# Two fused attention layers on one core: weight products, an early query and loads at two handovers put in another order

## The chip, the cores and the metric

The kernel runs on one core of a Trainium2 chip. A core has four compute engines that matter here: TensorE (PE) for matmuls, VectorE (DVE) and ScalarE (ACT) for elementwise work, GpSimd (POOL) for some elementwise work beside them; SyncE (SP) issues the transfers, which sixteen DMA engines carry out. Each engine works through its own queue of instructions in order, and semaphores make it wait for others. On-chip memory is SBUF, matmuls write to PSUM, and inputs, outputs and what is kept between stages lie in HBM.

The metric is the device time of one execution in microseconds (us), as the median of the runs. Lower is better.

## The reference, cut to what matters

The input x is 8 images of 256 channels with 64 by 64 pixels, all in float32. Two layers follow each other.

```
# layer 0
xr   = conv(x, w_sr, stride 4, 4x4 kernel)            # 256 channels, 16x16
xr   = (xr - mean_c) / sqrt(var_c + eps) * g + b      # over channels
q    = w_q x ; k, v = split(w_kv xr)                  # 8 heads of 32
x    = x + gamma * w_out softmax(q k^T / sqrt(32)) v  # 4096 queries, 256 keys

# layer 1
qkv  = w_qkv x                                        # 768 channels
agg  = grouped_1x1(depthwise_5x5(qkv))                # 96 groups of 8 channels
ms   = concat(qkv, agg)                               # heads of 3 x 8 channels
q, k = relu(ms.q), relu(ms.k) ; v = [ms.v, 1]
att  = q (k^T v) ; att = att[:-1] / (att[-1] + eps)   # linear attention, per head
x    = x + batchnorm(w_proj att)
```

## The kernel before, in words

The work is written for a tile framework: the program asks for tiles out of pools (a tag and a number of buffers say when a tile's memory is reused), and the framework's scheduler sets the order of the instructions on each engine and the semaphores between them. So the order in the source is a wish, and the built order can differ: independent work is pulled ahead. Where the memory of an earlier pass is taken again by a later one, the first use of it waits for the last use before it, transfers included. All transfers of the kernel are issued on SP's one queue; a transfer waits, besides for its data and its place, for the landing of the transfer eight places before it.

There are three passes, which hand their results on through HBM.

**The first pass** (`first_pass`) does layer 0 and the qkv product of layer 1. Its loop runs over steps n, 32 for each image: a strip of 512 pixels (`NG` = 8 for each image), a half of the channels, a half of the keys. A step computes scores on PE (L784) and their exponentials on ACT (L790), the values (`valued`, L808), the sum of the two key halves on POOL (`joined`, L819), the denominators (`counted`, L824), and `normed` on DVE: a transpose `rden` (L836), a reciprocal, a transpose `rall` (L839) and the product `att` (L841). `added` multiplies by the output weights (PE, L856), adds x (DVE, L857) and stores x. Every second strip `differences` and seven `qkv` products (PE, L900) follow, whose results are taken out of PSUM by DVE (`part`, `whole`, `stage`) and stored as k, v and `planes`. `keys_values` (L694 to L760) is a generator: it does the strided convolution with weights `wsr`, the normalisation (mean, var, rs) and keys and values; for the first image it runs before the loop, for the others in pieces within the image before. `queries` (L769, L777) makes q for a strip and a half: two matmuls and a copy by ACT.

`conv_weights` is another generator. It makes the weights of the second pass: for each of four groups it loads `wd` (L668), adds (L670), and makes eight products `wb` (L674, DVE, 128 x 1536) with one buffer, each of which is stored to HBM (`wt`). Each call of `next(weights, None)` makes one product, 32 in all. `border(b)` stores zeros to the rims of v in HBM, four transfers for each image.

**The second pass** (`second_pass`) does the depthwise and pointwise part as matmuls, and the sums k^T v. It runs over 64 units (t, k, b). A unit loads weights `w` (`load_weights`, L1130), pixels `d` (`load_cells`, L1136), and tokens `kq` and `vq` (`load_tokens`, L1143 and L1153). `paired` makes differences `c` of d (two on DVE, L1163 and L1164, and a copy on POOL, L1167). `convolve(u, 1, i)` is L1227 with d's of k and v, `convolve(u, 0, i)` is L1231 for q; ACT copies one of three banks to `both` (L1234), DVE adds it to the others (`s`, L1243), ACT makes `r` (L1244). `positive` is the relu of kq (L1210), `summed_raw` (L1253) and `summed` (L1270) are the sums, `ended` and `spread` (L1313 to L1330) turn them into the block matrix `bd`, `applied` (L1344 to L1356) makes the attention of agg, `stored` (L1364) stores it. `taps` are the weights with which `summed` is multiplied; taps_0 is for units of t = 0 (the first 32), taps_1 for t = 1.

**The third pass** (`third_pass`) makes the attention of qkv and the projection, in 64 steps. `loads(n)` loads raw pixels (L1473), x (L1482) and at some steps sums and agg (L1450, L1493); `vec` (L1515) and `wproj` (L1517) are loaded once. `flat` is a relu by ACT (L1506), `applied` is n (PE, L1541), den and tok (DVE, L1546), `turned` is a transpose on PE (L1559) with a copy by ACT (L1560), `proj` is p (PE, L1577), z (ACT, L1586) and y (DVE, L1595).

A check of the softmax's sums at the first pass's end decides whether a slower, general program has to run behind the third pass; it doesn't for these inputs.

The functions that the diff touches, and what calls them:

## Time and profile before

| | us |
|---|---|
| runs of the kernel | 3958.32, 3962.27, 3964.38 (median 3962.27) |
| the profiled execution | 3960.62 |
| its span | 3958.8 |
| PE busy | 3876.3 |
| VectorE busy | 2271.4 |
| ScalarE busy | 1517.6 |
| GpSimd busy | 1296.6 |
| first pass, roughly | 0 to 2076 |
| second pass, roughly | 2035 to 3303 |
| third pass, roughly | 3289 to the end |

The passes overlap by some work. The profile is that of one execution; a busy share is an average over all three passes, so what one edit is worth is read from the waits and windows around its own place. The profile's windows give, for a stretch of time, the busy time of each engine, the clock granted to PE as a share of the full one, and how busy the DMA engines were.

### The profile page before, as it was taken

Reading aid. Unit: us, or ns where it says so; the run is one execution under the profiler, and the core shown is the slowest. Engines: PE = TensorE matmul, PEld = TensorE weight load, DVE = VectorE, ACT = ScalarE, POOL = GpSimd, SP = SyncE. Lnnn points to the kernel's source line nnn. Section 1 sums busy time; section 2 is a strip of 40 time slices with the busy share of each in tenths; the row PEclk is TensorE's granted clock in tenths of the full one; section 3 lists DMA queues with packets and bytes.
Section 4 is the critical chain, followed back from the end, with each engine's and each line's share of the span. In section 5 each row is a group of like instructions: output and inputs, shape, how many; then the busy total and the mean of one; then the engine's idle time right before and its main releaser. Section 6 shows DMA issues by size and latency. Waiting matters only on the chain. (4 is left out here: it accounts for less than half of the span.)

```text
span 3958.8 us, 70047 instructions
## 1 busy us (share of the span) xinstructions
PE 3876.3 (98%) x27074; PEld 2277.0 (58%) x27074; DVE 2271.4 (57%) x3752; ACT 1517.6 (38%) x3473; POOL 1296.6 (33%) x1394
## 2 busy tenths in 40 slices
PE   8999999999999999999998999999999998999998
PEld 4443534434344343443346888888888885555555
DVE  3667465564655646556674666666666664444443
ACT  2344344443444434444432222222222223544444
POOL 2334343343433424334433444444444440000000
PEclk9999999999999999999998999999999999999999
DMA  7656354353443534444549887878778747777774
GB/s 246 188 176 201 101 140 129 96 154 99 136 132 98 149 104 129 136 115 116 135 117 265 247 225 221 231 221 229 230 214 230 206 144 198 225 210 222 209 223 141
DMA packets 570039, 691.35 MB, mean 175 GB/s; under 512 B 60128, under 2 KB 429280, under 8 KB 565600
## 3 DMA queue, kind: packets, MB, share of 16 engines
q1 hardware_dynamic: 569696, 686.78, 60.8%
q8 instruction: 215, 3.52, 0.4%
q14 instruction: 128, 1.05, 0.1%
HBM read 412.54 MB, written 274.10 MB: 173 GB/s over the span
## 5 line engine op out<-in xcount | busy, mean ns | idle before, releaser
L819 POOL TENSOR_TENSOR e<-e,e 128x512 f32<-128x512 f32 x512 | 682.1, 1364 | 931.5 <-PE av L808 864.1
L790 ACT ACTIVATE e<-sc 128x512 f32<-128x512 f32 x1024 | 531.0, 602 | 799.1 <-PE sc L784 794.4
L1227 PE MATMUL cv<-w,c 128*128 128x128 f32 x3072 | 386.9, 280 | 10.9 <-POOL c L1167 10.5
L1227 PEld LDWEIGHTS cv<-w,c 128*128 128x128 f32 x3072 | 361.2, 193 | 41.4 <-issue 29.3
L1595 DVE TENSOR_TENSOR y<-z,xs 128x256 f32<-128x256 f32 x256 | 142.7, 644 | 323.7 <-ACT z L1586 303.7
L784 PE MATMUL sc<-q,kk 32*128 32x512 f32 x2048 | 318.5, 640 | 1.5 <-DVE part L969 1.0
L1270 PE MATMUL sums<-vq,r 128*32 128x288 f32 x4096 | 307.3, 411 | 0.1
L900 PE MATMUL qkv<-differences,combined 128*128 128x512 f32 x576 | 304.8, 620 | 0.9 <-ACT e L790 0.7
L916 DVE TENSOR_TENSOR whole<-part,qkv 128x512 f32<-128x512 f32 x256 | 175.3, 687 | 189.3 <-PE qkv L900 179.0
L1244 ACT ACTIVATE r<-s 128x512 f32<-128x512 f32 x256 | 160.9, 628 | 306.8 <-DVE s L1243 300.0
L808 PE MATMUL av<-e,vv 128*32 128x512 f32 x2048 | 272.7, 604 | 1.9 <-ACT att L828 1.9
L1577 PE MATMUL p<-att,wproj 128*128 128x512 f32 x512 | 249.7, 610 | 9.6 <-DMA wproj<-in_w_proj_dram 5.6
L1586 ACT ACTIVATE z<-p,bn 128x256 f32<-128x256 f32 x256 | 133.8, 578 | 314.4 <-PE p L1577 240.7
L1231 PE MATMUL cv<-c,w 128*128 128x128 f32 x2048 | 253.1, 277 | 1.0 <-DVE s L1243 1.0
L856 PE MATMUL o<-att,wout 128*128 128x512 f32 x512 | 234.9, 600 | 10.8 <-DVE att L841 10.8
L769 PE MATMUL q<-x,wq 128*128 128x512 f32 x512 | 244.3, 599 | 0.0
L697 PE MATMUL sr<-x,wsr 128*128 128x256 f32 x1024 | 234.7, 384 | 8.4 <-DMA wsr<-in_w_sr_dram 8.4
L1577 PE MATMUL p<-agg,wproj 128*128 128x512 f32 x512 | 242.3, 595 | 0.0
L1231 PEld LDWEIGHTS cv<-c,w 128*128 128x128 f32 x2048 | 239.5, 192 | 1.2 <-DVE s L1243 1.2
L697 PEld LDWEIGHTS sr<-x,wsr 128*128 128x128 f32 x1024 | 196.5, 192 | 61.6 <-issue 33.8
L1234 ACT COPY both<-cv 128x512 f32<-128x512 f32 x128 | 75.0, 586 | 409.0 <-PE cv L1227 355.5
L1243 DVE TENSOR_TENSOR s<-cv,both 128x512 f32<-128x512 f32 x256 | 172.1, 672 | 86.4 <-PE cv L1231 43.3
(143 smaller groups left out, 6031.6 us busy)
## 6 DMA issues: line engine op xcount, KB each, us to landing
vq<-v SPq DMA_DIRECT2D x256, 384.0 KB
planes<-stage SPq DMA_DIRECT2D x128, 578.0 KB
d<-planes SPq DMA_DIRECT2D x128, 578.0 KB
raw<-planes SPq DMA_DIRECT2D x128, 272.0 KB
x<-in_xp_dram SPq DMA_DIRECT2D x64, 512.0 KB
wsr<-in_w_sr_dram SPq DMA_DIRECT2D x128, 256.0 KB
x<-x SPq DMA_DIRECT2D x128, 256.0 KB
k<-turned SPq DMA_DIRECT2D x256, 128.0 KB
```

The costliest lines, as they stand in the source:

```text
L697: nc.tensor.matmul(ps[:, oc], w[:, ci, oc * P : (oc + 1) * P], strips(b, f // 2)[:, ci, f % 2 * NK : (f % 2 + 1) * NK], start=(f == ci == ...
L769: nc.tensor.matmul(ps, consts["wq"][:, ci, c * P : (c + 1) * P], strips(b, s)[:, ci], start=(ci == 0), stop=(ci == 1),)
L784: nc.tensor.matmul(scs[h], kks[b][rows, c, kc * P : (kc + 1) * P], qs[rows], start=True, stop=True)
L790: nc.scalar.activation(e, scs[h], AF.Exp, scale=D0**-0.5)
L808: nc.tensor.matmul(sums["av"][cols], vvs[b][:, kc, c * P + h * D0 : c * P + (h + 1) * D0], es[h], start=(kc == 0), stop=(kc == 1),)
L819: nc.gpsimd.tensor_tensor(es1[h], es0[h], es1[h], ALU.add)
L856: nc.tensor.matmul(ps, consts["wout"][:, c, oc * P : (oc + 1) * P], att[c], start=(c == 0), stop=(c == 1))
L900: nc.tensor.matmul(ps, w, x, start=True, stop=True)
L1227: nc.tensor.matmul(out, x, m, start=(da == 0), stop=(da == 1))
L1231: nc.tensor.matmul(out, m, x, start=(da == 0), stop=(da == 1))
L1270: nc.tensor.matmul(ps[h * D0 : (h + 1) * D0, : 36 * D1].rearrange("p (r n e) -> p r n e", r=3, e=D1), kt[:, par, h, 2 * r + c], vq[:, r : ...
L1577: nc.tensor.matmul(ps.rearrange("p (f q n) -> p f q n", f=4, q=4), wproj[:, j, oc * P : (oc + 1) * P], src, start=(j == 0), stop=(j == 3),)
```

## The change

Four places are changed.

- In the first pass the queries of strip 0's second half are made within the chain of the first keys, between two pieces of `keys_values`, and no longer in the loop's step 0.
- `next(weights)` is called in steps above 32 where n % 8 is 3 or 6, and no longer in each of steps 0 to 31. The zeros of image 0 are asked for at step 20 instead of 2.
- At the second pass's start the loads of w0 (four), of taps_1 and of unit 2's tokens move from ahead of the loop, and the loop's first lines, to unit 0 behind `load_cells(2, 1)`.
- In the third pass the pools for data and flattened tiles are asked for ahead of the pool of constants, so each gets another place in memory.

In the order as built, 24 of the 32 weight products stand in the steps of image 0 and eight in those of image 1, where before all 32 stood in image 0. On SP the second pass begins d0_0, d1_2, kq_2, vq_2 (four), w0 (four), taps_1; before, it began taps_1, w0 (four), d0_0, d1_2, a w1, kq_2, vq_2 (four). On DVE the `c` of unit 6 stands behind two `s` of unit 2 that it stood ahead of. vec and wproj are issued between the last two loads of d while the second pass still runs, and no longer between its last two stores of attention; on PE the first two matmuls of n for step 1 stand ahead of the first p.

```diff
-    first = queries(0, 0, 0)
+    q = {0: queries(0, 0, 0)}
+    next(ahead)
+    q[1] = queries(0, 0, 1)
     for _ in ahead:
         pass
...
-    q, es = {0: first}, {}
+    es = {}
...
-        if n < n_all and kc == 0 and n + 2 < n_all:
+        if 0 < n < n_all and kc == 0 and n + 2 < n_all:
             q.pop(n // 2 - 1, None)
             q[n // 2 + 1] = queries(*order[n + 2][:3])
...
-        next(weights, None)
+
+        if n > 32 and n % 8 in (3, 6):
+            next(weights, None)
         if n < n_all:
             b, at = n // 32, n % 32
-            if at == 2:
+            if at == (20 if b == 0 else 2):
                 border(b)
...
     load_tokens(1)
-    for g in range(4):
-        load_weights(0, 0, g)
-
     def load(home, src, name):
...
-    for t in range(2):
+
+    def load_taps(t):
         taps.append((more if t else w_taps).tile([P, 4, 36, D1], F32, tag="taps", name=f"taps_{t}"))
         nc.sync.dma_start(taps[t], a.w_taps[:, 4 * t : 4 * t + 4])
+
+    load_taps(0)
...
-        if 0 < u < n_all - 1:
+        if 1 < u < n_all - 1:
             load_tokens(u + 1)
...
         if u + 2 < n_all:
             load_cells(u + 2, 1)
+        if u == 0:
+            load_tokens(2)
+            for g in range(4):
+                load_weights(0, 0, g)
+            load_taps(1)
...
+    data, flattened = (ctx.enter_context(tc.tile_pool(name=name, bufs=2)) for name in ("data3", "flattened3"))
     const = ctx.enter_context(tc.tile_pool(name="const3", bufs=1))
-    data, flattened, results = (
-        ctx.enter_context(tc.tile_pool(name=name, bufs=2)) for name in ("data3", "flattened3", "results3")
-    )
+    results = ctx.enter_context(tc.tile_pool(name="results3", bufs=2))
```

## The prediction

> **What bounds the kernel now.** I read the page's busy table first, then TensorE's (PE's) waits, then what each engine does around the longest waits, then short windows with clock and DMA share.
>
> ```profile
> span 3958.8 us, 70047 instructions
> PE 3876.3 (98%) x27074; PEld 2277.0 (58%) x27074; DVE 2271.4 (57%) x3752; ACT 1517.6 (38%) x3473; POOL 1296.6 (33%) x1394
> ```
>
> PE is busy 98%. The change takes no matmul away, so all it can win is PE's idle time, 3958.8 − 3876.3 = 82.5 us, and the time that PE works at half clock after a stall. PE's waits:
>
> ```profile
> PE o L856 <- DVE att L841: 10.8, 4, 6.1
> PE cv L1227 <- POOL c L1167: 10.5, 2, 9.5
> PE raw L1253 <- ACT kq L1210: 5.7, 1, 5.7
> PE p L1577 <- DMA wproj<-in_w_proj_dram: 5.6, 1, 5.6
> PE p L1577 <- ACT att L1560: 4.1, 2, 2.9
> PE var L721 <- DVE sq L715: 1.6, 1, 1.6
> ```
>
> The first lies in batch 0 of the first pass; the second and third where the second pass begins; the next two where the third begins; the last in the first keys' chain. In the timeline of VectorE (DVE), which gives start, length, operation and what ended the idle time before it:
>
> ```profile
> 70.74 2.54 DVE L674 TENSOR_TENSOR wb<-wd,wsmall 128x1536 f32<-128x1536 f32 x1 [0.20 <-DMA wt<-wb]
> 79.53 2.27 DVE L674 TENSOR_TENSOR wb<-wd,wsmall 128x1536 f32<-128x1536 f32 x1 [6.25 <-DMA wt<-wb]
> 81.73 0.70 DVE L836 STREAM_TRANSPOSE rden<-den 128x512 f32<-128x512 f32 x1
> 83.57 1.13 DVE L841 TENSOR_TENSOR att<-att,rall 128x512 f32<-128x512 f32 x1
> ...
> 110.28 0.69 DVE L670 TENSOR_TENSOR wd<-wd 128x512 f32<-128x512 f32 x1 [6.87 <-DMA wd<-in_w_big_dram]
> 111.00 1.76 DVE L674 TENSOR_TENSOR wb<-wd,wsmall 128x1536 f32<-128x1536 f32 x1
> 112.68 0.71 DVE L836 STREAM_TRANSPOSE rden<-den 128x512 f32<-128x512 f32 x1
> ```
>
> A weight product `wb` heads DVE's queue, waits there for the store of the one before (one buffer), and holds the softmax's last steps (rden to att) behind it. PE's output matmuls start at 84.75 (3.18 us idle) and 115.27 (6.08 us idle). Windows, whose columns are length, busy time by engine, granted clock, DMA share and GB/s:
>
> ```profile
> 84.70:88.70 4.00, 3.94 (x5) 1.65 (x6) 2.82 (x2) 0.00 (x0) 1.13 (x1) 0.57 0.29 66
> 112.00:120.00 8.00, 4.73 (x6) 1.60 (x6) 5.63 (x8) 2.09 (x7) 0.00 (x0) 0.57 0.48 169
> 2084.00:2100.00 16.00, 6.54 (x62) 6.27 (x63) 3.22 (x4) 1.82 (x3) 4.68 (x6) 0.57 1.02 307
> 3303.00:3315.00 12.00, 6.41 (x17) 3.21 (x18) 1.14 (x5) 2.65 (x6) 0.70 (x1) 0.57 0.65 193
> ```
>
> Each long stall is followed by half clock. At the second pass's start the DMA engines are full (1.02); at the third's they are not (0.65).
>
> **The change, part by part.** The sums are against the profiled execution (3960.62 us); the median of the runs is 3962.27, 1.65 more, and gains carry over.
>
> *First keys' chain.* q[1] is two matmuls (L769, about 0.6 us each) that stood among step 0's scores; they now stand between mean and var, where PE idles 1.65 us. Cover for 1.2 us; ScalarE's (ACT's) copy of q (some 0.6 us) goes ahead of `wide` and may cost 0.2. Gain **1.0** (0 if the copy delays `wide`; 3 if the half clock after this chain, 2.9 us in 44 to 52, goes too).
>
> *Weights and zeros.* The same 4 loads, 4 adds, 32 products (1.76 us alone, up to 2.8 beside POOL) and 32 stores. In the built order 24 products still stand in batch 0 and 8 in batch 1 (before: all 32 in batch 0), so the scheduler still hoists them, but fewer at a time. Between the first two atts the order was two products, now one, so the wait to 79.53 needn't stand before rden: den was ready at 76.73, rden to att takes 3.0, PE would start at about 80–81.6 instead of 84.75. Gain 3.2. The second: the reload of wd no longer stands before the fourth att, but two products do; den was ready at 102.43, two products with a landing between cost 2×1.8 + 4 to 5, so att ends at 111–113 instead of 115.2. Gain 2.3 to 4, I take 3. Against it: products now stand ahead of x and `whole`, which free PSUM banks for qkv; for two of them I charge 1 to 1.5 us each, 2.5 in all. For batch 1, where PE hardly waits today, nothing: DVE is busy 70 of 90 us late in the first pass, the eight products are 14–20 us spread over it; if that cover is missing, each costs its store's landing, up to 4–5 us. The zero stores of batch 0 go on SP ahead of the first wd load, 8 × 0.5 us; wd isn't wanted until the first att at 67: nothing.
>
> Here a rule bears. After the 3.18 us gap, the window 84.70–88.70 was granted 0.57: 43% of 4 us lost, **1.7 us**. The Trainium skill ("TensorE: Matmul & The Clock Gate", Part 1) has the clock halved after at least one idle window of about 3.4 us; by that a gap of 3.18 costs no dip and its end saves 3.2. By the row it saves 3.2 + 1.7 = 4.9. The rule also says that a shorter wait left over elsewhere is free of the dip. I go by the row: sub-3.4 gaps here do dip, so gaps that merely shrink keep theirs. The second gap's dip stays. Batch 0: 4.9 + 3 − 2.5 = **5.5** (0 to 12).
>
> *First to second pass.*
>
> ```profile
> 2081.50 1.07 POOL L1324 TENSOR_TENSOR bd<-rep,pix 128x512 f32<-128x512 f32 x1 [2.80 <-DMA taps<-in_w_taps_dram]
> 2092.52 1.24 POOL L1167 COPY c<-d 128x544 f32<-128x544 f32 x1 [6.54 <-DMA d<-planes]
> 2149.74 0.72 DVE L1163 TENSOR_TENSOR c<-d 128x544 f32<-128x544 f32 x1 [3.28 <-DMA d<-planes]
> ```
>
> taps_1 (0.58 MB) and four w0 loads (1.5 MB) leave their place ahead of d0_0 and d1_2 on SP. The first w0 load waited for all earlier stores to land (issue at 2081.41, 3.7 us after taps_1's) and everything on SP stood behind it; d1_2 went out at 2083.98 and landed at 2092.5. Now d1_2 can go out at about 2076.4: behind stores that land by 2081.4, with d0_0 ahead, 1.16 MB at 0.29 MB/us is 4.0 us: landing at about 2085.4. POOL's `bd` work (to 2086.0) is then the later one, as the same landings hold it; copy 1.24, PE at about 2087.3 instead of 2093.82. Gain **6.5**. Moved behind: w0_0 is first used at 2127, taps_1 later: covered by tens of us. Next late is the transfer backlog: the DMA engines are full from 2083 to 2150, and the end of that shows as 5.71 us of PE waiting for kq at 2155.84 (chain: d of unit 6 lands at 2149.74, c, s at 2153.53, r, relu of kq). The transfers start 3 to 4 us earlier, and in the new order both s stand ahead of that c on DVE, so s no longer waits for that load (3.3 us idle + 1.9 for the c pair). The kq is then 8.2 to 9.2 us earlier, PE 6.5: of the 5.7 some 2.5 go, and the 1.0 us that a cv waited for s at 2144.98. Dips (about 2.9 and 1.7 us) I leave in. Together **10** (3 if only the earlier transfers count, 14 with a dip gone).
>
> *Second to third pass.* vec and wproj (0.5 MB) go out between the last two d loads, over 30 us earlier, under steady work. p's wait for wproj (5.56) goes, but two matmuls of n(1) now stand ahead of the first p in PE's queue and need raw_1, which landed at 3313.03; its load was behind wproj and the att store, issued at 3302.77. It can now go out at 3299.8, and without 0.5 MB ahead at 0.19–0.2 MB/us (2.6 us) lands at about 3308.5–3309.5. So the wait changes name: gain 0 to 1 there. Later loads are 2.6 us earlier: the 2.85 us wait for ACT's att at 3326.52 (held by raw_3's landing) goes, perhaps its dip (1.7). Gain **3.5** (0 to 8). The batch-norm preparation now runs on DVE near 3256, where it idles 1.5 us: at most 1 us.
>
> Sum: 1.0 + 5.5 + 10 + 3.5 = **20**. 3960.6 − 20 = 3940.6 in the profiled execution, **3942** as a median.
>
> **The rivals.** *(a) The waits change their names.* At the second pass DMA is full, so an earlier cv only waits later, in raw or s, and keeps the 3.5 us of earlier transfers; in the third, raw_1 takes wproj's place (1.5); in batch 0 two products still stand before an att (2); start 1. Sum 8: **3954**. For it: share 1.02–1.05 and 24 of 32 products still in batch 0. Against: a steady second-pass unit takes 18.9 us and moves some 13–15 us of transfers, so the backlog drains.
> *(b) The dips go too.* If gaps cut below 3 us leave the clock alone, add 2.9 + 1.7 there, 2.9 at the start, 3–4 in batch 0, 2.6 + 1.7 in the third pass, about 15: **3927**. For it: the rule; against: the 3.18 us row.
> *(c) Slower: products in full steps.* Each product waits at DVE's head for a landing (17 waits cost DVE 43.4 us in 0–400, 2.55 each); ahead of `whole` and x they hold PSUM banks and PE stops in qkv. Over 32 products, 0.6 us of PE each (20 us) eats the gain and 0.87 us each (28 us) makes it slower by over 0.2%; at 1 us each the time is 3942 + 32 = **3974**. For it: no spare PE time in batch 1; against: `whole` waits for PE today (7.5 us in 15 waits in 0–400), not PE for it.
>
> **How the numbers follow.** Chances: the forecast 0.63, (a) 0.20, (b) 0.10, (c) 0.05, other 0.02. A measurement here tells about 0.2% (7.9 us) from no change, so faster is below 3954.3. (a) sits on that line: two thirds of it faster. Faster 0.63 + 0.10 + 0.13 = 0.86, same 0.08, slower 0.06. The forecast's own range is 3934–3950; with (a) and most of (b), 3928 to 3955.
>
> **What would show it.** Right: no 3-us gap at PE's second o group near 81; the cv wait for POOL near 2 to 3.5 us; c of unit 6 behind two s on DVE; the wait for kq about 2 us; wproj gone from PE's waits, with n (L1541) waiting for raw in its stead; PE's idle sum near 63–66 us. Wrong: new PE waits of qkv for `whole` or x in 60–600 (c), or cv and raw waiting for DMA by as much as was won (a).

## The result, and the profile after

The changed kernel takes 3956.34 us (median of 20 runs, 3950.82 to 3961.41). In the same session the kernel before took 3963.20 us (20 runs). The ratio is 0.9983 with a 95% interval of 0.9976 to 0.9989, so the gain is 6.9 us (4.4 to 9.5). It is real, but it lies inside the 0.2% that the prediction called "no change". The forecast was 3942, a gain of 20. The rival nearest to the result is (a), the waits change their names, at 3954.

The profiled execution took 3955.74 us. The page of the changed kernel begins:

```profile
span 3954.0 us, 70041 instructions
PE 3873.1 (98%) x27074; PEld 2276.1 (58%) x27074; DVE 2266.0 (57%) x3752; ACT 1516.9 (38%) x3473; POOL 1300.0 (33%) x1394
```

Span less PE busy is 80.9 us; it was 82.5. The forecast had 63 to 66. TensorE's waits after the change (in all, times, longest, in us):

```profile
PE raw L1257 <- ACT kq L1214: 8.1, 3, 6.0
PE sr L697 <- DMA wsr<-in_w_sr_dram: 8.1, 3, 5.5
PE at L1567 <- DVE tok L1554: 6.9, 3, 3.4
PE o L856 <- DVE att L841: 6.2, 3, 4.4
PE n L1549 <- ACT q L1514: 5.2, 1, 5.2
PE cv L1231 <- POOL c L1171: 5.1, 2, 4.1
PE sc L784 <- DVE whole L916: 4.8, 2, 2.5
...
PE av L808 <- ACT att L828: 3.1, 1, 3.1
```

The three waits that the change was aimed at are smaller or gone: o for att 10.8 to 6.2, cv for POOL 10.5 to 5.1, wproj (5.6) away. But raw's wait for kq has grown from 5.7 to 8.1, at's wait for tok from 3.4 to 6.9, and n for q, sc for `whole` and av for att (1.9 before) are new or longer. The sum hardly moved.

To see where the time went I cut each profiled execution at four matmuls that every kernel here has: the last one of the first pass (A is the time up to there), the first of unit 62's cv for q (B), the first p of step 10 of the third pass (C), and the end (D). The first matmuls of the second pass stand before the last ones of the first, so A holds a little of the second pass as well. The expectations below count the units of these stretches from cv to cv: what they call the first cv of unit 63 is the mark B, and their unit 1 and unit 5 begin with the first cv of the source's unit 2 (the one that waits for c of d1_2) and unit 6.

| | A | B | C | D | span |
|---|---|---|---|---|---|
| before | 2058.1 | 1217.5 | 141.8 | 541.4 | 3958.8 |
| after | 2055.2 | 1214.5 | 143.2 | 541.0 | 3954.0 |
| difference | −2.9 | −3.0 | +1.4 | −0.4 | −4.8 |
| forecast | −6.5 | −10 | −3.5 | 0 | −20 |

One execution says little about 1 or 2 us: kernels below that have the same code in a part differ there by up to 8 us in A, 6 in B and 5 in C. Where several kernels share a part, I give the mean over them too.

### The profile page after: what moved, and what is told of

Its sections match the earlier page's. It is cut to its first block, busy times and chain, and to the rows that moved or that the text cites. A ratio compares the mean times of both kernels' runs of the same rounds, so it can differ in the third digit from the quotient of the medians.

```text
span 3954.0 us, 70041 instructions
## 1 busy us (share of the span) xinstructions
PE 3873.1 (98%) x27074; PEld 2276.1 (58%) x27074; DVE 2266.0 (57%) x3752; ACT 1516.9 (38%) x3473; POOL 1300.0 (33%) x1394
```

## The experiments

The runs of each experiment were compared with runs of the kernel before on the same chip, whose medians lie between 3962.3 and 3964.4. "Ratio" is always to those, with its 95% interval.

### The first pass: which part wins?

**The weights put back** (the changed kernel without its weights and zeros part).

```diff
-        if n > 32 and n % 8 in (3, 6):
-            next(weights, None)
+        next(weights, None)
...
-            if at == (20 if b == 0 else 2):
+            if at == 2:
```

> The changed kernel with its weight products and zeros put back (one product asked for in each of steps 0 to 31, zeros at step 2). Theory: moving the products won 5.5 us in image 0 and lost 3.7 in image 1, the latter because loads of wsr stand behind stores of wt on SP. Then, against the changed kernel, the stretch from the first scores to those of image 1 is some 5 us longer (253.4 becomes about 258.5) and the next one, up to step 16 of image 1, some 3.5 us shorter (127.4 becomes about 123.7), with the wait for wsr (1.9 us) gone; the total 1 to 2 us longer than the changed kernel, some 5 to 6 shorter than before. Rival: the loss in image 1 has to do with the early query or chance; then the second stretch stays at 127.

Measured: 3966.19, ratio 1.0008 (1.0000 to 1.0016). Without this part the change is worth nothing. From the first scores to those of image 1 it took 269.3 us in the profile, where 258.5 was expected; the next half image took 123.6, as expected. The early query alone, below, shows what the 269.3 is.

**The weights alone** (the kernel before with this part and nothing else).

```diff
-        next(weights, None)
+        if n > 32 and n % 8 in (3, 6):
+            next(weights, None)
...
-            if at == 2:
+            if at == (20 if b == 0 else 2):
```

> The kernel before with the asking for weight products and zeros moved as in the change, nothing else. If the parts add (whole change 6.9 us shorter, early query 4.5 longer, loads 1.7 shorter, pools 2 longer): 9 to 12 us shorter than before. By the forecast's own step: 5.5 us shorter. If what the weights win depends on the early query (both change the order that the scheduler builds): 0 to 4 us shorter.

Measured: 3956.61, ratio 0.9980 (0.9971 to 0.9988). The part alone is worth 7.8 us, as much as the whole change. The other three parts together show no gain.

**The early query alone** (the kernel before, with q[1] made inside the first keys' chain).

```diff
-    first = queries(0, 0, 0)
+    q = {0: queries(0, 0, 0)}
+    next(ahead)
+    q[1] = queries(0, 0, 1)
...
-        if n < n_all and kc == 0 and n + 2 < n_all:
+        if 0 < n < n_all and kc == 0 and n + 2 < n_all:
```

> The kernel before with the query of strip 0's second half in the keys' chain, nothing else. By the forecast: 1 us shorter than before. By what the first experiment showed (weights at their old place with the early query): the stretch from the first scores to those of image 1 is 268 to 270 instead of 258.8, total 2 to 10 us longer than before. If the first experiment's 269 came from elsewhere: 258 to 259.

Measured: 3966.79, ratio 1.0012 (1.0006 to 1.0019): slower by 4.5 us. The forecast was a gain of 1.0. In its profile A is 2061.2 (before 2058.1), with no single wait that would carry the difference. On VectorE, ScalarE and SP its order of instructions differs from that of the kernel before only up to 142 us, and yet 3.4 of the 6.5 us between the two profiles lie behind the first pass: the profiles don't locate the loss. The stretch from the first scores to those of image 1 takes 260.4 us, not 268 to 270, although the kernel with the weights put back has the same order of instructions in its whole first pass. TensorE was at half clock for 13.7 us of this stretch here and for 34.1 there, so most of the 269.3 belongs to that one execution.

**One product a strip, in its place.** In the built order the products were still pulled ahead: 24 of 32 stand in the steps of image 0. This edit to the changed kernel makes one product in every fourth step and tells the scheduler to keep it in the written order, right behind a step's `att`.

```diff
-                nc.vector.tensor_tensor(
+                wb_ins = nc.vector.tensor_tensor(
...
+                tc.keep_in_program_order(wb_ins)
...
             normed(*order[d][:3])
+            if n > 4 and n % 4 == 3:
+                next(weights, None)
...
-        if n > 32 and n % 8 in (3, 6):
-            next(weights, None)
```

> The changed kernel with the products truly spread: one in each fourth step from step 7 on, put right behind the att product of that step on VectorE, so its store has some 33 us to land. Theory (a product at the head of VectorE's queue that waits for a store, and the loads queued behind that store on SP, are all that the weights cost): VectorE waits for wt near 0 instead of 42.5 us, PE's waits o for att and sc for whole between 60 and 300 go (some 10 us with their half clock), image 1 has no wait for wsr from this; first pass 5 to 10 us shorter than in the changed kernel (2032 becomes 2022 to 2027). Rival (VectorE has no room for the products themselves, 1.8 to 2.8 us each): new waits of about 0.5 us at each of 32 strips, first pass as long or longer than in the changed kernel.

Measured: 3952.30, ratio 0.9975 (0.9967 to 0.9983), 4.0 us below the changed kernel by the medians, with intervals that overlap a little.

**The same edit alone, on the kernel before** (the zeros stay at step 2).

> The kernel before with the weight products alone spread, one a strip behind att as in the second experiment; queries, loads at both handovers and pools as before. Theory (at both handovers the transfers end last, so the order of loads and pools is worth next to nothing, and the first pass is all): first pass about 2025 to 2027, the total 8 to 10 us shorter than before, as with the other parts added. Rival (the handovers are worth their waits, 3 us or more): 4 to 6 us shorter than before.

Measured: 3953.32, ratio 0.9979 (0.9972 to 0.9986). This edit alone wins at least as much as the whole change.

What the three orders do on VectorE can be read from its timeline (start, length, operation, idle time before it and what ended it). The changed kernel, around the second and the fourth att of image 0:

```profile
74.81 1.76 DVE L674 TENSOR_TENSOR wb<-wd,wsmall 128x1536 f32<-128x1536 f32 x1 [3.56 <-DMA wt<-wb]
76.48 0.71 DVE L836 STREAM_TRANSPOSE rden<-den 128x512 f32<-128x512 f32 x1
...
102.51 1.76 DVE L674 TENSOR_TENSOR wb<-wd,wsmall 128x1536 f32<-128x1536 f32 x1 [4.12 <-DMA wt<-wb]
104.18 0.71 DVE L836 STREAM_TRANSPOSE rden<-den 128x512 f32<-128x512 f32 x1
```

A product still heads the queue and waits for a store's landing ahead of rden. TensorE in the same kernel:

```profile
79.98 2.84 PE L856 MATMUL o<-att,wout 128*128 128x512 f32 x6 [0.46 <-DVE att L841]
...
94.50 1.94 PE L808 MATMUL av<-e,vv 128*32 128x512 f32 x8 [3.09 <-ACT att L828]
...
107.21 4.54 PE L856 MATMUL o<-att,wout 128*128 128x512 f32 x6 [4.42 <-DVE att L841]
```

The 3.18 us stall has gone, but a step later av stops for 3.09. The landings that VectorE waited for, from the view of the tile `wt`, before and then after:

```profile
  DVE wb L674: 43.4, 17
```

```profile
  DVE wb L674: 42.5, 18
```

The sum of these waits is unchanged. With one product a strip on the changed kernel the product starts when the att ahead of it ends:

```profile
106.79 0.69 DVE L842 TENSOR_TENSOR att<-att,rall 128x512 f32<-128x512 f32 x1
107.40 2.83 DVE L674 TENSOR_TENSOR wb<-wd,wsmall 128x1536 f32<-128x1536 f32 x1
```

Its store has a whole strip of time to land, and the view of `wt` shows no wait of VectorE at all.

Idle time alone doesn't tell the price of a product at the head of the queue. From the first scores to those of image 1 TensorE has nearly the same count of matmuls in all of these kernels. The windows of this stretch (length, PE busy and its count, PEld, DVE, ACT, POOL, clock, DMA share, GB/s), of the kernel before, the changed kernel, the changed kernel with the weights put back, and that with one product a strip:

```profile
52.15:310.99 258.84, 242.01 (x1017) 97.98 (x1016) 164.52 (x196) 103.27 (x242) 103.05 (x84) 0.97 0.59 186
```

```profile
51.09:304.45 253.36, 236.94 (x1014) 95.81 (x1013) 154.12 (x191) 102.00 (x241) 100.97 (x84) 0.96 0.56 170
```

```profile
51.93:321.23 269.30, 251.39 (x1014) 100.09 (x1013) 163.78 (x197) 103.20 (x241) 102.29 (x84) 0.94 0.57 180
```

```profile
51.63:276.54 224.91, 224.12 (x1014) 93.14 (x1013) 120.18 (x171) 101.31 (x241) 90.92 (x84) 1.00 0.44 127
```

All four hold the same matmuls, kind by kind, but for four of q that stand in this stretch in the kernel before alone. The last one is busy nearly throughout, at full clock: 224.1 us is what they take with five products among them. With the four of q it is 225.0, as the same edit alone on the kernel before shows (225.8 us, 0.8 of them idle, six products). So PE busy of the other three holds more than work. The trace's record of the clock gives the time at half clock, of which half is lost where PE is busy; what is then left over is time that matmuls wait inside a group, with no idle time on record.

| us | length | products | idle | lost at half clock | waiting inside groups | the rest |
|---|---|---|---|---|---|---|
| before | 258.8 | 29 | 16.8 | 5.4 | 11.6 | 225.0 |
| after | 253.4 | 23 | 16.4 | 9.5 | 3.4 | 224.1 |
| weights put back | 269.3 | 30 | 17.9 | 15.1 | 12.2 | 224.1 |
| one product a strip | 224.9 | 5 | 0.8 | 0 | 0 | 224.1 |

(Lost at half clock is half of: 13.7 us of half clock less 2.8 of it idle; 20.5 less 1.6; 34.1 less 4.0. Waiting is the length less the other terms.) By the same working the waiting inside groups is 11.4 to 13.3 us in all five profiles with the products in the old order, and 3.1 to 5.5 in all nine with the new one, so this column is no accident of one execution. The last kernel is 34 us shorter in this stretch, but only 10 up to the end of the first pass. The 24 between are the price of its 27 later products (the kernel before has three there), and hardly anything shows it but a length. The same half image, of the kernel before and of that with one product a strip, which has four in it:

```profile
561.92:682.88 120.96, 120.56 (x536) 48.47 (x532) 72.35 (x108) 52.04 (x126) 47.71 (x50) 1.00 0.50 140
```

```profile
532.81:659.07 126.26, 125.06 (x537) 50.34 (x533) 82.50 (x113) 52.34 (x126) 52.59 (x50) 1.00 0.57 163
```

Idle time is 0.4 and 1.2 us, the clock is full, and the second takes 5.3 us longer. Without products the halves of an image take 127.3 and 121.0 us in every kernel here, within 0.3; with four each, 130.0 and 126.3 in this one: +2.7 and +5.3, or on average **1.0 us for a product**, though none of them waits for a landing. What carries this price was not separated: besides VectorE's time there is the store (DMA share 0.57 instead of 0.50), and GpSimd, which is busy 52.6 us instead of 47.7 with the same 50 instructions. In image 0 of the kernel before the price was (258.8 − (225.8 − 6 × 1.0)) / 29, about 1.3 us; 225.8 us and six products are those of the same edit alone. What spreading wins is the difference of the two prices.

How such waiting looks is seen with the weights put back, where one group of eight scores takes 4.55 us:

```profile
222.56 1.88 PE L769 MATMUL q<-x,wq 128*128 128x512 f32 x4
224.37 4.55 PE L784 MATMUL sc<-q,kk 32*128 32x512 f32 x8
228.85 1.94 PE L808 MATMUL av<-e,vv 128*32 128x512 f32 x8
```

At other places eight take 1.14. VectorE of the same kernel was held until 224.2 by a product that had waited for its landing for 5.70 us, ahead of `part` and `whole`, which empty PSUM:

```profile
221.47 2.72 DVE L674 TENSOR_TENSOR wb<-wd,wsmall 128x1536 f32<-128x1536 f32 x1 [5.70 <-DMA wt<-wb]
224.11 0.70 DVE L920 STREAM_TRANSPOSE turned<-whole 128x512 f32<-128x512 f32 x1
224.74 0.64 DVE L969 TENSOR_TENSOR part<-part,qkv 128x512 f32<-128x512 f32 x1
```

That this late work holds the scores fits the lines; no run isolated it, so how a product makes matmuls wait inside a group stays open.

### The first handover: where did 10 us go?

The forecast's first step is in the trace: d1_2 was issued at 2075.25, and TensorE's cv of unit 2 follows the last matmul of the first pass by 29.6 us instead of 35.7, 6.1 less (6.5 forecast). Then the changed kernel stalls again. VectorE:

```profile
2164.04 0.73 DVE L1167 TENSOR_TENSOR c<-d 128x544 f32<-128x544 f32 x1 [5.93 <-DMA d<-planes]
...
2166.43 0.67 DVE L1247 TENSOR_TENSOR s<-cv,both 128x512 f32<-128x512 f32 x1
...
2167.65 0.65 DVE L1247 TENSOR_TENSOR s<-cv,both 128x512 f32<-128x512 f32 x1
```

ScalarE, and TensorE:

```profile
2167.67 1.04 ACT L1214 ACTIVATE kq<-kq 128x1024 f32<-128x1024 f32 x1
```

```profile
2168.76 1.08 PE L1257 MATMUL raw<-vq,kq 128*32 128x32 f32 x64 [5.98 <-ACT kq L1214]
```

It is the chain that the prediction described for unit 6 (d lands, c, s, relu of kq, raw), one unit later: now c of unit 7, whose d was issued at 2152.15 and landed at 2164.0, stands ahead of the two s of unit 3. The DMA engines are full before it (length, busy by engine, clock, DMA share, GB/s); from 2180 to 2220 us, where TensorE is never idle, their share is 0.88:

```profile
2100.00:2152.00 52.00, 48.20 (x662) 40.39 (x662) 32.40 (x60) 13.20 (x24) 20.72 (x23) 1.00 1.00 261
```

**c behind s** (the changed kernel, c of units 7 to 10 issued behind both s of four units before; `s_ins` keeps these additions).

```diff
+            s_ins[u, what, i] = nc.vector.tensor_add(s, ps, both)
...
-        if u + 1 < n_all:
+        if u in (6, 7, 8, 9):
+            with tc.issue_after(s_ins[u - 3, 0, 1].ins):
+                paired(u + 1, 1)
+        elif u + 1 < n_all:
             paired(u + 1, 1)
```

> The changed kernel with c of units 7 to 10 put behind both s of four units before on VectorE, which s does not need. Theory A (the order on VectorE: c waits for d of unit 7, that landed at 2164, and s, r and kq stand behind it): the 5.98 us wait of raw for kq goes and its half clock of 6.8 us with it, some 6 to 8 us in all. Theory B (backlog: the transfers are full and PE waits for the next of them): the wait shows a few us later as cv waiting for c or raw for vq or kq; total gain 0 to 2 us.

Measured: 3954.32, ratio 0.9979 (0.9972 to 0.9986), against 0.9983 for the changed kernel. From the first cv of unit 2 to that of unit 6 it became 8.7 us shorter (80.7 instead of 89.4), from there to B 8.3 longer. The load is as late as before, and something else waits for it, `ng` here and raw in six short waits (5.7 in all):

```profile
2168.94 0.72 DVE L1167 TENSOR_TENSOR c<-d 128x544 f32<-128x544 f32 x1 [7.15 <-DMA d<-planes]
```

```profile
2172.91 2.21 PE L1348 MATMUL ng<-bd,r 128*128 128x144 f32 x8 [2.67 <-DVE tok L1353]
```

So here the order on VectorE mostly says which matmul pays. **More transfers** (the changed kernel, with taps_1 loaded again in each of units 1 to 4, 2.36 MB in all; the values are the same):

```diff
             load_taps(1)
+        if 1 <= u <= 4:
+            nc.sync.dma_start(taps[1], a.w_taps[:, 4:8])
```

> The changed kernel with 2.36 MB more to load in units 1 to 4 of the second pass (taps_1 is loaded again, once a unit; the output stays). Theory B, backlog: at 0.27 MB/us that is 8.7 us of transfers, of which what does not fit into slack before unit 9 shows as PE waits for kq, vq or c: the stretch from unit 0 to unit 63 of the second pass 4 to 9 us longer. If single waits and not the volume set the end: 0 to 2 us.

Measured: 3959.74, ratio 0.9998 (0.9990 to 1.0006). From the first cv of unit 0 to B it takes 1244.0 us instead of 1237.8, 6.3 more (eleven profiles with this load order and no such addition lie between 1235.4 and 1240.7); 2.36 MB at the 0.26 MB/us of the window above would be 9 us. Added transfers in these units are paid for, most of them. The reverse was tried twice. **Fewer transfers early** (one product a strip, with the weights of k = 1 loaded in units 4 to 9 instead of 0 to 7 and taps_1 in unit 12):

```diff
+        if u == 12:
             load_taps(1)
...
-        if now and u + B < n_all:
+        if 4 <= u < 8:
+            load_weights(B, 1, u - 4)
+        if 6 <= u < 10:
+            load_weights(B, 0, u - 6)
+        if now and B <= u and u + B < n_all:
```

> The changed kernel with the products spread as in the second experiment, and 2.1 MB of loads taken out of the first units of the second pass: the weights of k = 1 are asked for in units 4 to 9 instead of 0 to 7, taps_1 at unit 12. Theory B, backlog: unit 0 to unit 63 some 4 to 7 us shorter than with spread products alone (1237), total 3945 to 3949. If the volume in these units is not what binds: 1236 to 1238, total 3951 to 3953.

Measured: 3955.10, ratio 0.9982 (0.9976 to 0.9989), no better than one product a strip without it (0.9975); from unit 0 to B it takes 1239.1 us. **Both together**, this and c of units 6 to 11 behind s (the lines of both diffs above, with units 5 to 10 in the list):

> The kernel with spread products and later loads of the last experiment, and c of units 6 to 11 behind both s of four units before on VectorE. If volume and order have to be changed together: unit 0 to unit 63 of the second pass 1230 to 1234 (1239 with later loads alone, 1237 with c behind s alone), total 3945 to 3949. If landings set the end whatever the order: 1236 to 1239, total 3951 to 3955.

Measured: 3955.28, ratio 0.9986 (0.9979 to 0.9993). From unit 0 to B it takes 1241.2 us. Taking 2.1 MB out of the first units won nothing. So added volume costs, and removed volume doesn't pay.

**The load order alone** (on the kernel before):

```diff
-    for g in range(4):
-        load_weights(0, 0, g)
...
+        if u == 0:
+            load_tokens(2)
+            for g in range(4):
+                load_weights(0, 0, g)
+            load_taps(1)
...
```

> The kernel before with the order of loads at the first handover alone. If the parts act by themselves: the stretch from the first matmul of the second pass to that of unit 1 is 6 us shorter than before (58.9 becomes 52.9), the next four units 2 to 2.5 longer (87.1 becomes 89.5), everything else within 0.5 us; total 3 to 4 us shorter. If the later loss came from other parts of the change, the four units stay at 87.

Measured: 3961.11, ratio 0.9996 (0.9988 to 1.0004), at most 5 us and perhaps nothing. The first stretch fell to 53.1, as expected; the next took 86.4, and the loss came behind it (1097.5 up to B instead of 1094.7). The means over all profiled kernels say the same, five with the old load order against eleven with the new one in its plain form. The cv of unit 2 follows the first pass by 29.8 us instead of 36.0, so 6.2 are won; of these the next four units lose 2.3 (88.0 instead of 85.7) and the rest up to B 2.2 (1097.1 instead of 1094.9). B is 1214.9 instead of 1216.5: 1.6 us for the part that was to bring 10.

### The second handover: where did 3.5 us go?

The third pass's waits moved as forecast. TensorE of the changed kernel:

```profile
3304.17 1.33 PE L1549 MATMUL n<-kvm,q 128*128 128x144 f32 x4 [5.21 <-ACT q L1514]
```

```profile
3340.20 1.07 PE L1567 MATMUL at<-ident,tok 128*128 128x128 f32 x4 [3.05 <-DVE tok L1554]
```

raw_1 landed at 3303.3, n waits in the place of p, and the 2.85 us wait for att is gone. But 36 us later there is a wait that no step of the prediction had, and its cause stands on VectorE:

```profile
3328.99 0.69 DVE L1554 TENSOR_TENSOR tok<-n,den 128x512 f32<-128x512 f32 x1
3337.71 0.30 DVE L1459 TENSOR_TENSOR kvp<-kvp 128x132 f32<-128x132 f32 x1 [8.03 <-DMA kvp<-kv]
...
3339.45 0.69 DVE L1554 TENSOR_TENSOR tok<-n,den 128x512 f32<-128x512 f32 x1
```

The addition of the sums of image 1, needed only at step 8, has been pulled ahead of y and tok of step 3, and waits 8 us at the queue's head for its load, which went out at 3331.7.

**The homes alone** (the kernel before, with the pools of the third pass in the new order):

```diff
+    data, flattened = (ctx.enter_context(tc.tile_pool(name=name, bufs=2)) for name in ("data3", "flattened3"))
     const = ctx.enter_context(tc.tile_pool(name="const3", bufs=1))
...
```

> The kernel before with the order of pools of the third pass alone. If the parts act by themselves: the stretch of the second handover is 1.4 us longer than before (141.8 becomes 143.2): the wait for wproj (5.6) is replaced by one for q of step 1 (5.2), the 2.85 us wait at 3326 goes and one of 3 us for tok with its half clock comes at about 3345. Total 0.5 to 2 us slower than before. If the gain of 3.5 that was forecast is there and another part eats it, 138.

Measured: 3965.05, ratio 1.0006 (0.9999 to 1.0013). C is 141.6, as before (141.8). The mean over the profiles is 144.3 in nine kernels with the new homes (141.6 to 146.4) and 142.7 in five with the old ones (141.7 to 144.0), so the homes cost rather than win. Additions of sums are pulled ahead with the old homes as well. In the kernel before, the first of them stands at 3346.1 and waits 0.47 us; in the kernel with the load order alone VectorE was held like this:

```profile
3345.71 0.30 DVE L1456 TENSOR_TENSOR kvp<-kvp 128x132 f32<-128x132 f32 x1 [5.10 <-DMA kvp<-kv]
```

**The sums of image 1 loaded early** (the changed kernel, right behind the loads of step 0):

```diff
-        if cls == 0 and half == 0:
+        if cls == 0 and half == 0 and b != 1:
             load_sums(b)
...
     loads(0)
+    load_sums(1)
```

> The changed kernel with the two small loads of image 1's sums (kvp, 16.5 KB each) issued behind the first loads of the third pass instead of behind those of step 7. Theory (these loads, which landed at 3337.7 behind larger ones, hold VectorE's queue and with it tok): the 3.05 us wait of at for tok at 3340 and the half clock after it (1.7 us) go; the stretch of the second handover (143.2) becomes 138 to 140. Rival (backlog of the transfers, not these two): another wait of 2 to 4 us takes its place within 20 us, the stretch stays within 1 us.

Measured: 3954.85, ratio 0.9979 (0.9971 to 0.9987); C is 143.9, no shorter. The sums of the next image have taken the place:

```profile
3337.79 0.30 DVE L1459 TENSOR_TENSOR kvp<-kvp 128x132 f32<-128x132 f32 x1 [4.09 <-DMA kvp<-kv]
```

**The first projection early** (both projections of step 0 ahead of n of step 1, so that p doesn't stand behind raw_1), and **both of these**:

```diff
+                if n == 1:
+                    tc.keep_in_program_order(relu)
...
+        if n == 1:
+            turned(*last)
+            last = None
+            flat(1)
+            proj(0, 0)
+            proj(0, 1)
...
```

> The changed kernel with both projections of step 0 put ahead of n of step 1 on PE, and ACT's relu of raw 1 behind the second copy of att. Theory A: the 5.21 us that PE waits for q of step 1 hold up to 5 us of projections, and PE arrives earlier at everything after; but sums of image 1 (kvp) still hold VectorE to about 3337.7, so most of it comes back as a longer wait of at for tok: gain 0 to 1.5. Theory B: nothing behind is late, gain 4 to 5 us.

Measured: 3955.63, ratio 0.9980 (0.9972 to 0.9989); C is 142.9.

> Both: projections of step 0 early, and the sums of image 1 loaded early. By theory A the two together win 7 to 9 us against the changed kernel (143.2 becomes 134 to 136), more than their single gains added; if the transfers as a whole are late, as much as the sums alone (3 to 5).

Measured: 3954.60, ratio 0.9977 (0.9968 to 0.9985); C is 143.4. In this order VectorE has y ahead of den and tok and waits for z, and at waits in its turn, 6.1 us near 3315. Neither told anything about the cause.

**Half the x loads left out** (the changed kernel; the third pass loads only the first 128 channels of x and adds them to both halves, so what it computes differs):

```diff
-        for c in range(2):
+        for c in range(1):
...
-                xs[:, oc, 2 * i : 2 * i + 2].rearrange("p f (y x) -> p f y x", x=NB),
+                xs[:, 0, 2 * i : 2 * i + 2].rearrange("p f (y x) -> p f y x", x=NB),
```

> The changed kernel with half of the loads of x in the third pass (256 KB of some 1.5 MB a step are left out, and the first half of the channels is added to both halves, so the output is another). Theory B, backlog: the stretch of the second handover 143.2 becomes 138 to 140, with fewer waits of at for tok after 3310. If it is a chain of latencies: within 1 us of 143.

Measured: 3949.17, ratio 0.9968 (0.9958 to 0.9978); C is 137.6. This left two readings: the volume of the transfers sets C, or the sums' load just arrives earlier when less is in front of it.

**The sums kept in their place** (the changed kernel; only the additions, of images 1 to 7, are held in the written order on VectorE):

```diff
-        nc.vector.tensor_add(kvp[:, :, :2], kvp[:, :, :2], kvp[:, :, 2:])
+        half_sums = nc.vector.tensor_add(kvp[:, :, :2], kvp[:, :, :2], kvp[:, :, 2:])
+        if b:
+            tc.keep_in_program_order(half_sums)
```

> The changed kernel with the additions of the sums (kvp, images 1 to 7) kept on VectorE in their written place, so that none is pulled ahead. If a load of sums at the head of VectorE's queue is what makes the third handover's new wait (at for tok near 3340, 3.05 us), that wait goes and the stretch from unit 63's first cv to p of step 10 is 139 to 141 us. If the volume of transfers behind the handover sets it, the wait turns up elsewhere and the stretch stays at 143 to 145 (changed kernel 143.2). Total: first case 3952 to 3954, second 3955 to 3957.

Measured: 3948.51, ratio 0.9960 (0.9947 to 0.9974). C is 138.1, 5.2 us below the changed kernel and 3.7 below the kernel before. No transfer was taken away. But the built order of the loads moved with the additions: between 3331 and 3348 us the changed kernel issues ten loads of sums (66 KB each by the trace, not 16.5 as written above), this one four. The loads of image 1's sums go out at the same place in both, from 3331.7 and from 3333.0, so the 8 us that VectorE stood still were the order on VectorE. What share the six later loads have in the 5.2 us was not separated. Windows over the same 15 us, of the changed kernel and then of this one:

```profile
3330.00:3345.00 15.00, 11.95 (x42) 7.42 (x41) 5.58 (x16) 4.96 (x12) 0.00 (x0) 0.89 0.87 156
```

```profile
3330.00:3345.00 15.00, 15.00 (x58) 8.57 (x57) 6.37 (x12) 8.02 (x20) 0.00 (x0) 1.00 0.82 180
```

The 3.05 us of idle time are gone, and with them the half clock behind it. Together they make up most of the 5.2.

### The parts that pay, together

The kernel before with one product a strip, the load order and the homes, without the early query (the diffs of these three above, put together):

> The kernel before with one product a strip, the new order of loads and of pools, but the query at its old place. If the early query costs 4.5 us in any company: 3946 to 3950. If its cost came from the products beside it, which are spread here: 3951 to 3954, as with it.

Measured: 3952.88, ratio 0.9970 (0.9959 to 0.9981). The same with the query early (and the zeros at step 20) was 0.9975 (0.9967 to 0.9983): next to spread products the query's loss of 4.5 us doesn't show, though the intervals leave room for it. The last run adds the three lines that keep the sums in their place:

> The kernel before with one weight product a strip, the new load order, the new homes of the third pass and the sums kept in their written place; the early query is left out. If the sums' place costs 3 to 4 us of the third handover: 3948 to 3951. If not: as without it, 3952 to 3953.

Measured: 3946.92, ratio 0.9956 (0.9942 to 0.9969), with A 2050.9, B 1214.5, C 138.4, D 540.9. It is 17 us below the kernel before and the fastest kernel of this study; next to the sums in order alone (0.9960) its lead is inside the intervals.

## Why the prediction was wrong, point by point

The part that failed most is the first handover. The prediction let an earlier start of the loads end as a gain of 10 us, and 1.6 to 3.0 of it were left. The first pass came near its 6.5 us (5.7 as a mean), for other reasons than the forecast's, and the second handover brought none of its 3.5.

**First keys' chain, gain 1.0: wrong.** The cover was there: TensorE's idle time up to the first scores fell from 11.5 to 8.9 us, and the wait of var for sq is gone. The time up to the first scores fell by 1.1 in the two profiles, but 0.9 of it stand ahead of the first matmul, where nothing was changed. From the first matmul to the first scores the means over seven kernels without the early query and thirteen with it are 46.6 and 46.0 us (43.5 to 50.2), so q's matmuls found room. But with the rest of the kernel as it was, the edit cost 4.5 us (2.4 to 7.5). The step took the queue of TensorE for the whole of the cost and named only a delay of `wide`; what the moved copy and matmuls change in the steps behind was not costed. Which of them costs is open.

**Weights and zeros, gain 5.5: the size was near, the working was not.** Alone, this part measured 7.8 us (4.8 to 11.5). The forecast's own terms add up to 5.4. From the first scores to those of image 1 it is 253.4 us instead of 258.8, 5.5 less (5.8 in the means over eight kernels with the change and three with the old first pass). The first o wait fell by 2.7 (3.18 to 0.46; 3.2 forecast), the second by 1.7 (6.08 to 4.42; 3 forecast). Against that stand an av wait 1.2 longer and two sc waits for `whole` of 4.8 together (2.5 charged); all idle time fell by 0.4 only, and half clock lost 4.0 more where the prediction had 1.7 less. The gain is 8.2 us less of waiting inside groups, a term that the prediction didn't have, and 0.9 of q's four matmuls, which have moved ahead. Six products fewer stand in this stretch, which is 0.9 us each.

**"For batch 1 … nothing": too low, by 1 to 4 us.** The six products were not removed but moved. From the first scores of image 1 to those of its step 16 there are now eight and not two, and the stretch is 127.4 us instead of 123.7 in this profile. As a mean it is 125.7 in nine kernels with the new order of products (124.2 to 127.6) and 124.5 in five with the old one (123.6 to 125.2). The prediction looked at VectorE, where it saw room for 14 to 20 us, and said what a product costs only "if that cover is missing". Its 70 of 90 us are from the end of the pass; from 450 to 600 us VectorE was busy 91.6 of 150, so there was more cover than it thought. A product still costs TensorE something there, 1.0 us on average in the kernels with one a strip and 0.2 to 0.6 here. Part of it in this kernel goes by SP's queue, where the products' stores stand between the loads of `wsr` for the next image (start and length of each issue):

```profile
394.09 0.34 SPq L680 DMA_DIRECT2D wt<-wb  x1
394.56 0.59 SPq L694 DMA_DIRECT2D wsr<-in_w_sr_dram  x1
399.45 0.32 SPq L680 DMA_DIRECT2D wt<-wb  x1
399.86 0.58 SPq L694 DMA_DIRECT2D wsr<-in_w_sr_dram  x1
```

A load goes out 0.4 to 0.5 us behind each store, and a store only when its product is made. TensorE pays once:

```profile
429.87 1.99 PE L697 MATMUL sr<-x,wsr 128*128 128x256 f32 x8 [1.85 <-DMA wsr<-in_w_sr_dram]
```

Together with the first chain A is 2.9 us shorter in this profile, and 5.7 as a mean over eight kernels with the change against three with the old first pass; the forecast was 6.5.

**First to second pass, gain 10: this step failed.** Its first term, 6.5, was measured as 6.1 (6.2 in the means). The failing sentence is the next: "of the 5.7 some 2.5 go". The wait for kq didn't shrink, it grew to 5.98 and moved to the next unit, and half clock stayed with it; up to B only 3.0 us remain in the profile and 1.6 in the means, since the units up to 6 and those behind them lose 2.3 and 2.2 again. The prediction assumed that two s standing ahead of one c would free the chain, and looked at one c. The next c stands the same way, and where it was moved as well, the late load stopped `ng` and raw instead. This is rival (a) at its place ("keeps the 3.5 us of earlier transfers"), and the argument against it, a unit of 18.9 us that needs only 13 to 15 us of transfers, was too coarse: the DMA engines stayed full to 2152. Whether it is volume, the loads' places in SP's queue or the waits for landings ahead of them is open: more volume costs 6.3 us, but less volume, the other order and both together brought nothing.

**Second to third pass, gain 3.5: the waits moved as said, a queue was missed.** The wait for wproj went and that for att went. The step charged n for raw_1, and never asked what VectorE would pull ahead of tok in the new order. The additions of sums stood there, and C grew by 1.4 us in the profile (1.6 in the means). With the sums in their place C is 5.2 shorter than that (6.1 in the means of two and nine kernels), and 3.7 shorter than before. That this is the 3.5 of the forecast is not shown: sums are pulled ahead with the old homes too, and no run keeps them in place there.

**The rule and the row.** The prediction went by the row, a dip after 3.18 us, against the clock gate rule of about 3.4 us (the Trainium skill, "TensorE: Matmul & The Clock Gate", Part 1). The changed kernel's windows right behind gaps of 0.46, 3.09 and 1.85 us, and last the kernel before, behind its wait of 1.22 us for wsr at 204.65:

```profile
79.98:83.98 4.00, 4.00 (x14) 1.66 (x14) 3.15 (x3) 0.01 (x1) 3.81 (x2) 1.00 0.30 74
94.50:98.50 4.00, 4.00 (x24) 0.91 (x24) 2.82 (x2) 2.40 (x5) 0.51 (x1) 0.61 0.56 174
429.87:433.87 4.00, 4.00 (x25) 1.92 (x25) 2.71 (x5) 0.92 (x2) 0.00 (x0) 1.00 0.43 148
204.65:208.05 3.40, 3.40 (x8) 2.75 (x9) 2.96 (x6) 0.00 (x0) 0.00 (x0) 0.50 0.90 294
```

The 3.09 us gap got 0.61 although it is shorter than 3.4, as the row of the 3.18 us gap did; so the prediction was right not to go by the rule. But the row is no rule either: the 1.85 us gap got no dip, and the 1.22 us gap did. Rival (b) wanted the dips gone where gaps are cut below 3 us. That happened at the first o wait, and yet half clock lost 4.0 us more in image 0.

**Rival (c)**, products in full steps, had the price right: "at 1 us each". It was charged to all 32 as new, and so gave 3974; but the products had cost about 1.3 each where they stood. The prediction took that old price for zero beyond the two o waits.

**The range** (3928 to 3955) missed by 1.3 us. Rival (a), at 3954, was given 0.20; in the kernel before, a DMA share of 1.04 from 2100 to 2152 us spoke for more.

## What to carry to other kernels

Work that is moved off a crowded place is not free at the new one: measure its price in a stretch that repeats (here the half images, 1.0 us on average for a product) and forecast the difference of the two prices. When one wait is cut, list on each in-order queue the instruction that will now stand at its head with a load outstanding, since a scheduler fills freed time with early work: here additions of 0.3 us, kept in their place, were worth about as much as the whole change. At a handover with full DMA engines, don't count an earlier start as a gain before you have followed the late loads to the last of them: here 6.2 us won at the start were 1.6 us at the end.

## What the hardware showed

PE's busy share hides stalls: of the 242 us that PE was busy in the first image of the kernel before, 11.6 were matmuls waiting inside their groups, found only because another order ran the same matmuls in 225.0 us. Half clock can follow such hidden waits: in the kernel with the weights put back it began at 227.3 us, within the group of scores shown above, ahead of which no idle time is on record for 18 us. Its image 0 had 34.1 us of half clock against 13.7 before, at nearly equal idle time (17.9 and 16.8 us), and the kernel with the early query alone, with the same order of instructions, had 13.7 (17.7 us idle). Much of what executions of one order differ by is half clock. Of the two kernels with one product a strip and the early query whose A differs most (2047.8 and 2055.1 us, with one order in the first pass), the longer one had two intervals of 6.8 us at half clock, behind gaps of 0.83 and 0.81 us, and the shorter none up to the end of A; half of 13.7 is 6.8 of the 7.3 us. The half-clock intervals in these traces are 3.4, 6.8, 10.2 or 13.7 us long, and the open gap doesn't tell which: 3.4 us at the 4.42 us gap before 107.21, 6.8 at the 2.53 us gap before 221.52, both in the changed kernel.
